# Fetching the rows of eleven steps one by one on SP in a graph network kernel

## The chip, the core and the metric

The kernel runs on one core of a Trainium2 chip. A core has five engines that work side by side, each with its own queue of instructions: TensorE (PE, whose weight loads the profile lists apart as PEld), VectorE (DVE), ScalarE (ACT), GpSimd (POOL) and SyncE (SP). [...] DMAs are issued from these queues too: here SP and ACT issue plain transfers, and POOL issues indirect ones, in which a list of row numbers says where each of 128 rows comes from. The metric is the device time of one execution in microseconds.

## What is computed

There are 6250 nodes with 256 features and 100,000 edges, sorted by their target `dst`; an edge has 64 features. Two layers follow each other, each added to its input and normalised:

```python
e   = relu((x[dst] - x[src]) @ theta_w.T + theta_b + x[src] @ phi_w.T + phi_b)
out = segment_max(e, dst)                  # first layer, 0 where a node has no edge
x   = layernorm(x + out)
...
hv = x @ W_in + b_in                       # second layer, two rounds with own weights W, b
for W, b in ((W_u0, b_u0), (W_u1, b_u1)):
    m   = relu(concat(hv[src], edge_attr) @ W + b)
    msg = segment_max(m, dst)
    hv  = hv + where(has_in, msg, 0)
out = layernorm(x + relu(hv @ W_ro + b_ro))
```

In all three aggregations a node takes the maximum over its incoming edges of a row that depends on the source node alone, plus (in the two rounds) a product of the edge's own features. The part that depends on the source can therefore be computed once for each node and written to a table in DRAM; what remains for each edge is to fetch a row of 1 KB from that table and take part in a running maximum.

## The kernel before

`sweep(r)` makes one of three passes, r = 0 for the first layer and 1 and 2 for the two rounds. The edges are laid out as 128 lanes of 782 steps, so that a step is 128 edges, one on each partition. Steps are gathered in groups of eight (K = 8), and a group has one tile `run` of 128 x 8 x 256 floats, 1 MB, out of a ring of nine such buffers. The steps also form 14 blocks (thirteen of 56 steps, one of 54), within which the running maximum goes on from step to step.

A step goes through these stations:

- **POOL** fetches the 128 source rows from `table[r]` with one indirect DMA into the step's slot of `run` (`sources`, L798). The function `gathered` says how far these gathers run ahead: about 41 steps, five groups. In pass 0, 40 steps take another way and have no gather in this place.
- **PE** computes, in passes 1 and 2, the products of the edge features for two steps at a time (`pair`, L833) from a tile `hT`, which ACT loads for a whole group, three groups ahead (`features`, L822).
- **DVE** adds those products to the fetched rows, two steps at a time (L1043), and takes the running maximum in place, one step at a time (L1056).
- **SP** stores the group's tile of running maxima to `S` in DRAM, 1 MB, when its eight steps are done (L1064).

At a block's end `over_lanes` carries maxima across lanes: PE transposes, ACT copies (`lim2`, L846), DVE scans, and ACT puts the result into `cs` (L865).

The 49 node tiles of a pass are placed between the steps by a plan worked out when the program is built. For each, POOL fetches the rows of `S` at which the tile's nodes end (`rows`, L878), and this gather waits for all S stores issued up to then. Then DVE and PE add what came in from other lanes (`picks`, L890, and `carried`, L897), DVE takes the maximum (L944), ACT the relu (L945), and products with the next weights follow (transposes L768, the copy `aT` on ACT L770, the product L776, `new` L956). ACT then stores the new rows into the next pass's table. SP loads `x` and `xT` for these tasks (L902, L906).

The plan fixes each engine's order. SP's queue thus holds an S store for each group and few things besides, POOL's holds the gathers, and ACT's holds the hT loads, the stores to the tables and to the output, and the small operations of node tiles and blocks.

The buffers of `run` are handed out by the pool in the order in which the tiles are asked for: the ninth request after a tile gets its buffer, and what writes there first waits until the store of the old content is done. Before the change a tile is asked for when the first gather of its group is issued (in `sources`).

Of the kernel before, what the change touches and what calls it, by code (L numbers as in the profile page):

```python
# [8 lines left out]
F32 = mybir.dt.float32  # L9
BF16 = mybir.dt.bfloat16  # L10
I32 = mybir.dt.int32
AF = mybir.ActivationFunctionType
OP = mybir.AluOpType
# [4 lines left out]
P = 128  # L18
N = 6250
D = 256  # L20
# [3 lines left out]
K = 8  # L24
# [19 lines left out]
TROWS = ROWS + 1  # L44
# [3 lines left out]
FIRM = K  # L48
AHEAD = 5 * K
RING = 9  # L50
KEPT = 7
SLACK = 600

# [15 lines left out]
def raw(s):  # L69

    i = s // K * 2 + s % K
    return i if s % K < 2 and i < RAW else None
# [13 lines left out]
def place(t):  # L86

    return P * (t - 1) if t else SPARE + 1
# [376 lines left out]
@with_exitstack  # L465
def gnn_kernel(
    ctx: ExitStack, tc: tile.TileContext, x, xT, src, dst, he, th_wT, th_b, ph_wT, ph_b,
    w_in, b_in, w_u0, b_u0, w_u1, b_u1, w_ro, b_ro, pos, heT, xTn, xn, w_inT, head, near, out,
):
    nc = tc.nc  # L470
    const = ctx.enter_context(tc.tile_pool(name="const", bufs=1))
    dram = ctx.enter_context(tc.tile_pool(name="dram", bufs=1, space=DRAM))
    table = [dram.tile([TROWS, D], F32, name=f"table{r}") for r in range(3)]
# [19 lines left out]
    part = const.tile([P, 1], F32)  # L493
# [18 lines left out]
    wt = const.tile([P, 2, D], F32)  # L512
    s_s = const.tile([P, FS], I32)
    s_r = const.tile([P, RAW], I32)
    s_e = const.tile([P, EARLY], I32)
    whole = const.tile([P, NB], F32)
    lim = const.tile([P, FS], F32)
# [3 lines left out]
    with tc.manual_schedule(), tc.tile_pool(name="pro", bufs=2) as pro, \  # L521
            tc.tile_pool(name="pro_ps", bufs=4, space=PSUM) as pps:
        nc.sync.dma_start(wd, ph_wT.rearrange("(k p) f -> p k f", p=P))
        nc.scalar.dma_start(wt, th_wT.rearrange("(k p) f -> p k f", p=P))
        dp = pro.tile([P, 2 * FS], I32, name="dp", bufs=1)
        d_s, p_s = dp[:, :FS], dp[:, FS:]
        nc.scalar.dma_start(s_r, near)
        for i in range(SOON):
            gather_raw(nc, x, h_sb, s_r, i)
        zero = pro.tile([1, D], F32, name="zero", bufs=1)  # L530
        nc.vector.memset(zero, 0.0)
        for r in range(3):
            nc.scalar.dma_start(table[r][SPARE:SPARE + 1, :], zero)
        parts = []
        for g in range(NT // PART):
            xg = pro.tile([P, 2, PART * P], F32, name="xg", bufs=NT // PART)
            nc.sync.dma_start(xg, xTn[:, :, g * PART * P:(g + 1) * PART * P])
            parts.append(xg)
            if g == 0:
                nc.sync.dma_start(dp, pos[:, 4 * NB:4 * NB + 2 * FS])  # L540
                nc.sync.dma_start(ends_sb.rearrange("p a b -> p (a b)"), pos[:, :4 * NB])
                nc.sync.dma_start(s_s, pos[:, 4 * NB + 2 * FS:])
        nc.vector.tensor_sub(wd, wd, wt)

        def check():
            down = pro.tile([P, FS], F32, name="down", bufs=1)
            nc.vector.tensor_tensor(down, p_s, d_s, OP.is_lt)
            downs = pro.tile([P, 1], F32, name="downs", bufs=1)
            nc.vector.tensor_reduce(downs, down, AX.X, OP.max)
            out_of = pro.tile([1, 2, NB], F32, name="out_of", bufs=1)  # L550
            nc.vector.tensor_tensor(out_of[:, 0, :], fd[0:1, :], floor, OP.is_lt)
            nc.vector.tensor_tensor(out_of[:, 1, :], fd[0:1, :], ceil, OP.is_gt)
            bad = pro.tile([1, 1], F32, name="bad", bufs=1)
            nc.vector.tensor_reduce(bad, out_of.rearrange("p a b -> p (a b)"), AX.X, OP.max)
            nc.vector.tensor_max(downs[0:1, :], downs[0:1, :], bad)
            breaks_p = pps.tile([P, 512], F32, name="breaks_p", bufs=1)
            nc.tensor.matmul(breaks_p[:, :1], every, downs, start=True, stop=True)
            nc.vector.tensor_copy(breaks, breaks_p[:, :1])
            keep = pro.tile([P, FS], F32, name="down", bufs=1)
            nc.vector.tensor_tensor(keep, p_s, d_s, OP.is_equal)  # L560
            alike = BLOCKS.count(BLOCKS[0])
            nc.vector.tensor_reduce(whole[:, :alike], keep[:, :alike * BLOCKS[0]].rearrange(
                "p (b s) -> p b s", s=BLOCKS[0]), AX.X, OP.min)
            for b in range(alike, NB):
                nc.vector.tensor_reduce(whole[:, b:b + 1], keep[:, FIRST[b]:FIRST[b] + BLOCKS[b]], AX.X, OP.min)
            nc.vector.tensor_scalar(lim, keep, 2.0 * BIG, -BIG, OP.mult, OP.add)
            bits = pro.tile([P, FS], I32, name="bits", bufs=1)
            nc.vector.tensor_scalar(bits, s_s, float(P), float(TROWS), OP.is_lt, OP.mult)
            nc.vector.scalar_tensor_tensor(s_s, s_s, float(-P), bits, OP.add, OP.add)
            nc.vector.tensor_scalar(s_e, s_s[:, :EARLY], float(SPARE), None, OP.min)  # L570
            nc.vector.tensor_scalar(bits, d_s, P - 1, None, OP.bitwise_and)
            nc.vector.tensor_copy(lo, bits)
            nc.vector.tensor_scalar(bits, d_s, 7, None, OP.arith_shift_right)
            nc.vector.tensor_copy(hi, bits)

        for g, xg in enumerate(parts):
            g0 = pro.tile([P, PART, D], F32, name="g0", bufs=3)
            for i in range(0, PART, 2):
                w = min(2, PART - i)
                ps = pps.tile([P, 512], F32, name="ps0")  # L580
                for q in range(w):
                    for k in range(2):
                        nc.tensor.matmul(ps[:, q * D:(q + 1) * D], xg[:, k, (i + q) * P:(i + q + 1) * P], wd[:, k, :],
                                         start=(k == 0), stop=(k == 1))
                put = g0[:, i:i + w, :].rearrange("p a f -> p (a f)")
                nc.scalar.copy(put, ps[:, :w * D])
            i = 1 if g == 0 else 0
            if i:
                nc.sync.dma_start(table[0][place(0):place(0) + P, :], g0[:, 0, :])
            at = place(g * PART + i)  # L590
            nc.sync.dma_start(table[0][at:at + (PART - i) * P, :].rearrange("(a p) f -> p a f", p=P), g0[:, i:, :])
            if g == 0:
                check()
# [10 lines left out]
def in_order(ctx: ExitStack, tc: tile.TileContext, g):  # L604
# [8 lines left out]
    nc = tc.nc  # L613
    table, ident, above, every, col, col_f = (g[n] for n in ("table", "ident", "above", "every", "col", "col_f"))
    whole, lim, lo, hi, s_s, fd, pd, ld, nd = (g[n] for n in ("whole", "lim", "lo", "hi", "s_s", "fd", "pd", "ld", "nd"))
    heT, xTn, xn, out = (g[n] for n in ("heT", "xTn", "xn", "out"))
    s_e, head, x, h_sb, wd, s_r, x1 = (g[n] for n in ("s_e", "head", "x", "h_sb", "wd", "s_r", "x1"))
    part = g["part"]
    ctx.enter_context(tc.manual_schedule())
    one = ctx.enter_context(tc.tile_pool(name="one", bufs=1))  # L620
    work = ctx.enter_context(tc.tile_pool(name="work", bufs=2))
# [11 lines left out]

    first = work.tile([P, 4, 2, D], F32, tag="run", name="first", bufs=RING)

# [35 lines left out]
    nc.vector.tensor_scalar(link, whole, 2.0 * BIG, -BIG, OP.mult, OP.add)  # L671
    cs = one.tile([P, KEPT, D + 2], F32, name="cs")
    nc.vector.memset(cs[:, :, D:], 1.0)
# [36 lines left out]
    for i in range(2):  # L710
        low.append(psum.tile([P, 512], F32, tag="he", name="low", bufs=5))
        n = min(half * K, FS - i * half * K)
# [66 lines left out]
    def sweep(r):  # L779
# [9 lines left out]

        runs = ahead.pop(r, {})  # L790

        def sources(s, r=r, runs=runs):
            if s % K == 0:
                runs[s // K] = work.tile([P, K, D], F32, tag="run", name="run", bufs=RING)
            if r == 0 and raw(s) is not None:
                return
            early = r > 0 and s < EARLY
            nc.gpsimd.indirect_dma_start(  # L798
                out=runs[s // K][:, s % K, :], out_offset=None, in_=table[r][:SPARE + 1, :] if early else table[r],
                in_offset=bass.IndirectOffsetOnAxis(ap=(s_e if early else s_s)[:, s:s + 1], axis=0))  # L800

        def raw_turn(i):

# [37 lines left out]
        def over_lanes(b, last):  # L841
# [18 lines left out]
            def back():  # L860
# [3 lines left out]
                carried_in.append(b)  # L864
                nc.scalar.copy(cs[:, b % KEPT, :D], cp[:, :D])  # L865

# [3 lines left out]
        def node(t, g, b):  # L870
# [22 lines left out]
            def carried():  # L893
                assert max(carried_in) - SPAN[t][0] < KEPT
                o["v"] = psum.tile([P, 512], F32, tag="v", name="v", bufs=1)
# [110 lines left out]
        for t in reversed(range(NT)):  # L1006
            e = max(FIRST[SPAN[t][1]] + BLOCKS[SPAN[t][1]], begin)
            b = max(b + (gap if b < FS else 3), e + 4, gathered(e) + 4)
            g = e
# [13 lines left out]
        for s in range(FS):  # L1023
# [4 lines left out]
            c, j = divmod(s, K)  # L1028
# [8 lines left out]
            if s % 2 == 0:  # L1037
# [6 lines left out]
                elif raw(s) is not None:  # L1044
                    sums = hp.pop(s // 2)
                    i = raw(s) // 2
# [7 lines left out]
            row = sums[:, s % 2 * D:(s % 2 + 1) * D]  # L1054
# [10 lines left out]
            if s == FIRST[blk] + BLOCKS[blk] - 1:  # L1065
                over_lanes(blk, prev)
                blk += 1
            for f, a in tasks.pop(s, ()):
                f(*a)
        for f, a in tasks.pop(FS):  # L1070
# [9 lines left out]
    for r in range(3):  # L1080
        sweep(r)
# [50 lines left out]
```

## Time and profile before

| | |
|---|---|
| median of three timed runs | 4156.62 us |
| lowest and highest of them | 4119.23 and 4168.13 us |
| the profiled execution itself | 4196.96 us |
| its span on the core | 4195.2 us |
| mean granted TensorE clock in it | 0.666 |
| busy: POOL, DVE, PE, ACT | 57%, 50%, 46%, 6% |
| S stores of a group (1 MB each) | 291 of 297 |
| data moved | 752.27 MB, 179 GB/s on average |

A row for a group of instructions gives source line, engine, operation, the tiles written and read, the shape, and the count; after the bar come the summed busy time in us and the mean of one in ns; after the second bar the time for which the engine had stood idle just before them, and what ended most of that time ("issue" where nothing in the profile shows a reason, "remote" where it was a semaphore that can't be put down to one instruction). SPq, ACTq and POOLq stand for the queues, in which loads of registers and issues of DMAs are listed. Source lines are those of the kernel before.

The 1.8 us between the span and the profiled time lie around the program. The profiled execution took 1% longer than the median of the timed ones, so sums made from its rows are made against 4196.96 us.

### The profile page before, as it was taken

How to read it: one execution, taken by the hardware profiler on the slowest of the kernel's cores; microseconds unless marked ns; L12 is line 12 of the kernel's file. 1: busy time of each engine (PE TensorE's matmuls, PEld its weight loads, DVE VectorE, ACT ScalarE, POOL GpSimd, SP SyncE). 2: the span in 40 equal slices, each digit the busy share in tenths (PEclk: the TensorE clock that was granted, in tenths of full speed). 3: DMA queues.
4: the chain of work that ended last, by engine and by line, in shares of the span. 5: the costliest groups of instructions: out<-in, count | busy, mean ns of one | idle time of the engine just before them, and what ended most of it. 6: DMA issues, size and time to landing. Idle time of an engine off the chain costs nothing. (4 is left out here: it accounts for less than half of the span.)

```text
span 4195.2 us, 21994 instructions
## 1 busy us (share of the span) xinstructions
PE 1921.7 (46%) x4631; PEld 844.2 (20%) x4631; DVE 2117.7 (50%) x4750; ACT 234.5 (6%) x618; POOL 2382.1 (57%) x2500
## 2 busy tenths in 40 slices
PE   5353223445442244454455455454444555555555
PEld 4232112111110111222211111121122222211111
DVE  1265556444444345455555544454455656555556
ACT  1000000111110000000000000000000000000000
POOL 5554555665556655566565555555555655555553
PEclk8665555655655566777776766677677777666667
DMA  6454546555555555555565555555555655555554
GB/s 232 134 179 145 169 141 211 167 186 182 185 176 205 177 161 181 175 187 188 170 202 172 186 183 172 169 192 176 174 182 180 194 189 194 177 181 178 185 182 154
DMA packets 261984, 752.27 MB, mean 179 GB/s; under 512 B 54725, under 2 KB 116914, under 8 KB 224594
## 3 DMA queue, kind: packets, MB, share of 16 engines
q0 software_dynamic: 119664, 326.92, 26.1%
q1 hardware_dynamic: 82672, 344.28, 22.3%
q10 hardware_dynamic: 59506, 79.59, 5.9%
q8 instruction: 39, 0.64, 0.1%
q14 instruction: 103, 0.84, 0.1%
HBM read 410.98 MB, written 339.59 MB: 179 GB/s over the span
## 5 line engine op out<-in xcount | busy, mean ns | idle before, releaser
L798 POOL DMA_INDIRECT run<-table,s_s x2258 | 2156.2, 955 | 903.4 <-issue 664.4
L833 PE MATMUL hp<-whe,hT 128*128 128x512 f32 x1564 | 1066.4, 775 | 669.2 <-DVE run L1056 244.4
L1056 DVE SCALAR_TENSOR_TENSOR run<-run,lim,hp 128x256 f32<-128x256 f32 x1573 | 754.8, 480 | 309.3 <-remote 128.1
L878 POOL DMA_INDIRECT m<-S,end_i x147 | 140.6, 957 | 833.8 <-DMA S<-run 368.7
L1043 DVE TENSOR_TENSOR hp<-hp,run 128x512 f32<-128x512 f32 x782 | 541.3, 692 | 140.9 <-remote 51.4
L833 PEld LDWEIGHTS hp<-whe,hT 128*128 128x128 f32 x1564 | 303.7, 231 | 1200.2 <-DVE run L1056 495.8
L1056 DVE SCALAR_TENSOR_TENSOR run<-run,lim 128x256 f32<-128x256 f32 x731 | 351.9, 481 | 125.2 <-remote 42.1
L897 PE MATMUL v<-cs,pick 128*128 128x256 f32 (+1 forms) x438 | 184.4, 540 | 258.3 <-issue 92.9
L768 PE MATMUL tp<-ident,h_sb 128*128 128x128 f32 x196 | 52.4, 360 | 416.9 <-DVE h_sb L948 219.9
L776 PE MATMUL prod<-wcat,aT 128*128 128x512 f32 x196 | 178.3, 1064 | 61.2 <-issue 44.0
L944 DVE TENSOR_TENSOR m<-m,v 128x256 f32<-128x256 f32 x98 | 40.6, 414 | 308.6 <-remote 248.0
L718 DVE TENSOR_TENSOR ol<-col,low 128x1024 bf16<-128x1024 bf16 x98 | 118.9, 1213 | 123.5 <-remote 110.3
L897 PEld LDWEIGHTS v<-cs,pick 128*128 128x128 f32 x438 | 105.0, 265 | 370.5 <-issue 260.0
L729 PE MATMUL hist<-oh,ol 128*128 128x8 bf16 (+7 forms) x782 | 34.7, 167 | 314.4 <-DVE oh L724 244.0
L945 ACT ACTIVATE m<-m,has 128x256 f32<-128x256 f32 x98 | 49.8, 508 | 1622.7 <-DVE m L944 1023.2
L768 PEld LDWEIGHTS tp<-ident,h_sb 128*128 128x128 f32 x196 | 24.0, 172 | 516.7 <-issue 471.4
L939 DVE TENSOR_TENSOR new<-prod,b 128x256 f32<-128x256 f32 x49 | 20.8, 424 | 167.8 <-PE prod L776 69.5
L729 PEld LDWEIGHTS <-ol 128*128 128x128 bf16 x782 | 36.0, 103 | 339.8 <-DVE ol L718 246.2
L956 DVE TENSOR_TENSOR new<-prod,bu 128x256 f32<-128x256 f32 x49 | 20.6, 421 | 163.3 <-remote 106.5
L776 PE MATMUL prod<-wu,aT 128*128 128x256 f32 x196 | 72.7, 509 | 60.7 <-ACT aT L770 31.7
L960 DVE TENSOR_TENSOR m<-prod,bro 128x256 f32<-128x256 f32 x49 | 20.7, 422 | 151.5 <-remote 99.2
L768 PE MATMUL tp<-ident,x 128*128 128x128 f32 x98 | 31.6, 424 | 142.7 <-DVE no L916 39.9
(133 smaller groups left out, 1486.0 us busy)
## 6 DMA issues: line engine op xcount, KB each, us to landing
S<-run SPq DMA_DIRECT2D x291, 1024.0 KB
hT<-in_heT ACTq DMA_DIRECT2D x196, 256.0 KB
run<-table,s_s POOLq DMA_INDIRECT x2258
table<-new ACTq DMA_DIRECT2D x98, 128.0 KB
xg<-in_xTn SPq DMA_DIRECT2D x7, 896.0 KB
xT<-in_xTn SPq DMA_DIRECT2D x49, 128.0 KB
x<-in_xn SPq DMA_DIRECT2D x49, 128.0 KB
x<-x ACTq DMA_DIRECT2D x49, 128.0 KB
```

The costliest lines, as they stand in the source:

```text
L718: nc.vector.tensor_tensor(ol[:, :k, :], col.unsqueeze(1).to_broadcast([P, k, P]), low[c // half][:, c % half * K:c % half * K + k].unsquee ...
L729: nc.tensor.matmul(hist[:, t0:t0 + w], ol[:, j, :], oh[:, j, :w], start=False, stop=(c == NG - 1 and j == k - 1))
L768: nc.tensor.transpose(tp[:, k * P:(k + 1) * P], a[:, k * P:(k + 1) * P], ident)
L776: nc.tensor.matmul(ps[:, :n], aT[:, k, :], w[:, k, :], start=(k == 0), stop=(k == 1))
L798: nc.gpsimd.indirect_dma_start(out=runs[s // K][:, s % K, :], out_offset=None, in_=table[r][:SPARE + 1, :] if early else table[r], in_offs ...
L833: nc.tensor.matmul(hp[i], hT[c][:, q, :], whe[r - 1].rearrange("p s f -> p (s f)"), start=True, stop=not early)
L878: i = nc.gpsimd.indirect_dma_start(out=o["m"], out_offset=None, in_=S_r[:P * (FIRST[SPAN[t][1]] + BLOCKS[SPAN[t][1]]), :], in_offset=bass. ...
L897: nc.tensor.matmul(o["v"][:, :N1], p, cs[:, blk % KEPT, :N1], start=(blk == SPAN[t][0]), stop=(blk == SPAN[t][1]))
L944: nc.vector.tensor_max(o["m"], o["m"], o["v"][:, :D])
L945: nc.scalar.activation(o["m"], o["m"], AF.Relu, scale=has[:, t:t + 1])
L1043: nc.vector.tensor_add(sums, sums, two)
L1056: nc.vector.scalar_tensor_tensor(cur, prev, lim[:, s:s + 1], row, OP.min, OP.max)
```

## The change

Eleven steps of each pass, named in `SIDE`, are the last steps of groups 10, 18, 26 and so on up to 90. POOL no longer gathers these: 33 gathers of the three passes are gone. Their 128 rows are fetched by SP in eight parts of sixteen. At the first step of every group from 2 to 89, behind the S store of the group before, SP loads sixteen row numbers from a small tile `side_sb` into registers, and then issues sixteen DMAs, each of which copies one row of 1 KB from the table to its partition of the step's slot. The eight parts of a step are thus spread over the eight groups ahead of its own. The tiles of these groups are asked for at the first part (`place_for`), because the slot must exist by then; before, a tile was asked for about five groups ahead.

The row numbers are prepared in the prologue, in the same way as those of the gathers: one more load by SP, and two small DVE operations. In this text `FusedRegOps` or FUSED_REGOPS is the instruction by which SP works out a DMA's address from the register.

```diff
+SIDE = [(8 * i + 10) * K + K - 1 for i in range(11)]
...
+    side_sb = const.tile([len(SIDE), P], I32)
...
+                nc.sync.dma_start(side_sb, side)
...
+            nc.vector.tensor_scalar(bits_b, side_sb, float(P), float(TROWS), OP.is_lt, OP.mult)
+            nc.vector.scalar_tensor_tensor(side_sb, side_sb, float(-P), bits_b, OP.add, OP.add)
...
+        def place_for(c, runs=runs):
+            if c not in runs:
+                runs[c] = work.tile([P, K, D], F32, tag="run", name="run", bufs=RING)
+
         def sources(s, r=r, runs=runs):
             if s % K == 0:
-                runs[s // K] = work.tile([P, K, D], F32, tag="run", name="run", bufs=RING)
-            if r == 0 and raw(s) is not None:
+                place_for(s // K, runs)
+            if r == 0 and raw(s) is not None or s in SIDE:
                 return
...
+        def rows_one_by_one(i, part_of):
+
+            s, n = SIDE[i], P // K
+            regs = [nc.sync.alloc_register(name=f"row{r}_{i}_{part_of}_{q}") for q in range(n)]
+            nc.sync.load(regs, side_sb[i:i + 1, part_of * n:(part_of + 1) * n])
+            for q, reg in enumerate(regs):
+                number = nc.sync.snap(reg, donate=True, min_val=0, max_val=TROWS - 1)
+                p = part_of * n + q
+                nc.sync.dma_start(runs[s // K][p:p + 1, s % K, :], table[r][bass.ds(number, 1), :])
...
+            if j == 0:
+                for i, to_come in enumerate(SIDE):
+                    if 0 < to_come // K - c <= K:
+                        for ahead_c in range(c + 1, to_come // K + 1):
+                            place_for(ahead_c)
+                        rows_one_by_one(i, K - (to_come // K - c))
             for f, a in tasks.pop(s, ()):
                 f(*a)
```

In program order the batch of a group thus stands on SP behind the store of the group before, and ahead of the loads of `x` and `xT` that belong to the same step. The orders of PE, ACT and DVE are otherwise the same, and POOL's differs by the missing gathers.

## The prediction

> **What bounds the kernel now.** I read the page first: the engines' busy rows, then the costliest groups, then the waits, then stretches of a pass. In the groups the last pair of columns is busy time with the mean of one, and idle time ahead with what ended most of it.
>
> ```profile
> PE 1921.7 (46%) x4631; PEld 844.2 (20%) x4631; DVE 2117.7 (50%) x4750; ACT 234.5 (6%) x618; POOL 2382.1 (57%) x2500
> ...
> L798 POOL DMA_INDIRECT run<-table,s_s x2258 | 2156.2, 955 | 903.4 <-issue 664.4
> L878 POOL DMA_INDIRECT m<-S,end_i x147 | 140.6, 957 | 833.8 <-DMA S<-run 368.7
> L1056 DVE SCALAR_TENSOR_TENSOR run<-run,lim,hp 128x256 f32<-128x256 f32 x1573 | 754.8, 480 | 309.3 <-remote 128.1
> L1043 DVE TENSOR_TENSOR hp<-hp,run 128x512 f32<-128x512 f32 x782 | 541.3, 692 | 140.9 <-remote 51.4
> ```
>
> No engine is full. POOL comes nearest: a gather is 0.955 us busy, and in the timeline the next starts 1.25 us after it (0.30 us "issue" between). All 2493 gathers make 3116 us of a span of 4195.2; most of POOL's other time is the 834 us ahead of the m gathers. There it waits for S stores:
>
> ```profile
> POOL m L878 <- DMA S<-run: 368.7, 29, 28.3
> ```
>
> So POOL has run ahead and waits for what DVE has just computed: it is not the last one. The gathers do run far ahead of DVE: `gathered` allows about 41 steps.
>
> What paces DVE shows in the windows (columns: PE, PEld, DVE, ACT, POOL busy, then granted clock, DMA share, GB/s):
>
> ```profile
> 2089.00:2123.00 34.00, 23.35 (x54) 8.14 (x52) 30.41 (x63) 1.76 (x4) 22.05 (x24) 1.00 0.84 290
> 2123.00:2198.00 75.00, 35.81 (x77) 15.96 (x77) 33.83 (x72) 4.14 (x11) 40.78 (x44) 0.68 0.48 156
> ```
>
> A pass alternates. In fast stretches DVE is 89% busy (30.41 of 34.00) at full clock, and a group of 8 steps takes 4 x (0.69 + 2 x 0.48) = 6.6 us. In slow ones the granted clock falls (0.68 here, 0.50 in the 58 us after), DVE is 45% busy and waits at node ends for PE, up to 24 us at a time ahead of L944. Through both, SP mostly waits for DVE. The next lines are SP's largest wait, from the waits of its own queue, and ten S stores of a fast stretch, from its timeline (start, length, count):
>
> ```profile
> SPq L1064 <- DVE run L1056: 1746.1, 132, 60.9
> ```
> ```profile
> 1538.74 60.77 SPq L1064 DMA_DIRECT2D S<-run  x10
> ```
>
> Nine intervals in 60.45 us are 6.7 us each. Over the 267 groups in which the change adds work (2 to 90 of each pass), the start times of L1064 give intervals of 3604 us in sum, 13.5 us on average; 143 of them are under 11 us. SP has little to do, but the change gives it a batch per group.
>
> **Removed.** 33 gathers on POOL (11 steps x 3 passes): 33 x 1.25 = 41 us of POOL's time. As POOL waits for DVE's stores, I take 0 on the path; bounds 0 and -41. The bytes stay: the same rows move.
>
> **Added on SP.** Behind each of 88 stores a pass: one load of 16 registers, 16 address computations, 16 DMAs of one row (1 KB). In all 264 loads, 4224 computations, 4224 DMAs, against some 500 DMAs on SP now. Nearest rows, from the views of two source lines (min/median/max ns):
>
> ```profile
> L595 SPq TENSOR_LOAD <-breaks x1: 510/510/510, 48.0 to 48.0; - x1
> L595 SPq FUSED_REGOPS  x1: 191/191/191, 48.6 to 48.6; - x1
> ```
> ```profile
> L533 ACTq DMA_DIRECT2D table<-zero x3: 233/313/592, 1.8 to 2.7; - x3
> ```
>
> The last is a DMA of one row too, and its issue costs what that of a 1 MB S store costs (0.320 us). Gaps between SP's instructions are about 0.06 us. A row is 0.191 + 0.313 + 0.06 = 0.56 us, 16 rows 9.0 us; with the store (0.32 us) and the load (0.51 us) a batch is B = 9.9 us.
>
> [...] The trace has loads of one register only[...]. By the row the sum below is about +110 us[...]. I take 0.6 us more than the row[...]: B = 10.5 us.
>
> The ring adds a wait: tiles for eight groups ahead are taken at once, so the first batch of every eight writes into the buffer whose S store was just issued, and SP stands until that has landed. In the trace's DMA records stores land 4.1 us after issue (mean; 3.4 to 5.3), so 33 batches take some 3.8 us more, 0.5 us on the average of all: B = 11. Lowest: if address and issue overlap, a row is 0.35 us; row eight of a batch waits for the store's landing anyway (below), so 4.1 + 9 x 0.35 = 7.3 us.
>
> **Who waits for SP.** The plain DMAs of SP and ACT share eight completion semaphores, taken in program order, and each waits until the one eight before it has landed. In the program after the change row 8 of a batch waits for the store, rows 9 to 16 for rows 1 to 8, and ACT's next transfer (the hT load of group c+3 at the start of group c) for the rows of the batch before. Behind that load in ACT's queue stand relu (L945), the aT copy (L770), lim2 (L846), cs (L865). So SP's lateness reaches PE through hT, and DVE through the last rows of the SIDE step. The hT load for c+3 waits for about the tenth row of batch c-1, which begins with group c-1; PE needs it when DVE begins group c+2, three groups or 19.8 us later. Ten rows of sixteen take 7 us and the landing 2 to 3 us, as the trace's small loads do, so SP may be late by about 10 us before DVE slows; 6 us if the last rows and landings take longer.
>
> **The sum.** I replay the 267 intervals: each store begins when DVE is ready or B after the one before, whichever is later, and what its lateness exceeds the tolerated lag by is added to DVE's delay. In lockstep (no lag) B = 9, 10, 11, 13 adds 201, 313, 446, 756 us; with 6 us of lag 68, 145, 241, 495; with 10 us 43, 79, 153, 378. For B = 11 I take the middle of 241 and 153: +197 us. The slow stretches hide the rest; were their cover gone, the lockstep figure would hold.
>
> ACT's 196 stores of table, x1 and out are also held inside a batch: at most 8 rows x 0.56 = 4.5 us, half on average, in 11 of 13.5 us: 196 x 2.25 x 0.8 = 353 us as upper bound, 0 as lower. Node tasks stand 6 steps apart and mostly absorb it: a tenth, +35 us. The prologue's one load and two small DVE operations on 11x128 cost under 1 us of DVE beside PE's start: 0 to +2, taken as 0. PE's instructions stay.
>
> Sum: 4197 (profiled run, 4195.2 span and 1.8 around it) + 197 + 35 = 4429 us. The median of the timed runs is 4156.62, 0.990 of the profiled run: 4429 x 0.990 = 4385 us.
>
> **Rivals.**
> A. Absorbed (the other side: not slower). Slow stretches come with a low granted clock after PE-heavy bursts. If that limits PE's average work, a burst slowed by SP is paid back by a shorter slow stretch. For: clock 1.00 in bursts, 0.5 to 0.68 between, on a total of PE work that doesn't change. Against: in the slow stretches node chains wait on each other, not on matmul throughput alone. It also decides where B is near 7.3 us: the replay gives under +75. Time 4157 to 4230, say 4180.
> B. Faster. Smoothed bursts let the clock stay high, and POOL's 41 us come off the path where it catches up. 4157 - 41 = 4116 from POOL alone; over 2% needs another 42 us of the clock. Against: DVE doesn't wait for gathers in the trace.
> C. Lockstep with costly loads. B = 13 and no tolerance gives +756, with 6 us of lag +495. For: ACT and SP are coupled in every group. 4157 + 0.99 x 495 = 4647, up to 4905; say 4700.
>
> **How the numbers follow.** The main case has 0.43 (4250 to 4500: with B from 10 to 12 at 10 and 6 us of lag +79 to +357, the ACT term 0 to 100); A 0.30, of which 0.04 above 4240; B 0.09; C 0.18. Two per cent (83 us) is about what a measurement of this kernel tells from no change, its runs spread by 1.2%. Faster by over 2% (under 4073): 0.08, from B. Within 2%: 0.27, from A and the rest of B. Slower: 0.65. The range leaves out most of B below 4105 and the upper part of C above 4800.
>
> **What would show it.** SP's rows: 4224 row DMAs of about 0.31 us and computations of 0.19; the 16-register load at 0.5 to 1.1 us (main)[...]. Store starts in fast stretches 10 to 12 us apart instead of 6.7; SP's wait for DVE falls far below 1746 us; PE's wait for hT and ACT's for DMAs appear; POOL's 2225 run gathers stay at 0.955 us and wait longer. The granted clock tells A: if it rises in the slow stretches and these shorten, the bursts were paid back. I am wrong if a row costs 0.35 us or less, if PE is truly limited on average, or if ACT's held stores reach the node chains in full.

## The result, and the profile after

The kernel after the change takes 5202.43 us (5200.02 to 5214.46), the kernel before beside it 4141.57 us: 1.256 times as long, with a 95% interval of 1.248 to 1.265. The direction was forecast and the size was not: 1061 us were lost where some 230 were expected, outside the range.

One thing has to be said ahead of all numbers. The experiments ran on several chips, and these are of two kinds: on some the kernel before takes 4141 to 4181 us, as in the runs above, on others 3179 us. Each experiment is therefore compared with the kernel before on its own chip. In the following the two kinds are called the slower and the quicker chips. Each chip of the experiments ran one batch of them and none came back, so whether the chip itself makes the difference, or something that held during its batch, the runs don't show.

The first rows are from the page of the kernel after: busy time by engine, then two groups with busy time, mean ns of one, and the idle time ahead with its main releaser. Line numbers are those of the kernel after: L808 are the gathers, L1063 the add, L1076 the running maximum, L1084 the S store, L816 the load of the sixteen row numbers, L820 the row DMAs.

```profile
PE 1871.7 (36%) x4631; PEld 850.9 (16%) x4631; DVE 2112.4 (41%) x4752; ACT 234.6 (5%) x618; POOL 2355.8 (45%) x2467
...
L808 POOL DMA_INDIRECT run<-table,s_s x2225 | 2128.8, 957 | 1253.1 <-issue 656.8
...
L1063 DVE TENSOR_TENSOR hp<-hp,run 128x512 f32<-128x512 f32 x782 | 541.0, 692 | 943.2 <-DMA run<-table 667.5
```

The engines are busy for about as long as before and wait longer. DVE's add now waits 667.5 us for rows of `run`. The waits of SP's own queue show who is late now:

```profile
SPq L1084 <- DVE run L1076: 217.8, 39, 54.0
SPq L820 <- DMA hT<-in_heT: 83.2, 45, 5.7
```

SP waited 1746 us for DVE before; of that 218 us are left. SP has become the engine on which the others wait. Its trace keeps one order throughout: in all 264 batches the store comes first, then the load, then the sixteen rows, and none of its 13,880 instructions starts before the one ahead has ended. Its instructions are listed by the views of two lines (min/median/max ns):

```profile
L816 SPq TENSOR_LOAD <-side_sb x264: 354/2747/3864, 158.3 to 5117.7; - x132
```
```profile
L820 SPq FUSED_REGOPS  x4224: 1/37/1397, 160.6 to 5130.6; - x192
L820 SPq MOVE run<-table x4224: 1/29/1403, 161.9 to 5130.7; - x192
L820 SPq DMA_DIRECT2D run<-table x4224: 1/228/1408, 161.9 to 5130.8; - x192
```

By the medians a row is 0.41 us with the gaps between instructions, and a whole undisturbed batch 9.8 to 10.4 us (store 0.36, load 2.75, sixteen rows 6.6), a little less than forecast. But the columns of extremes reach 1.4 us, even for a MOVE; 404 of the 4224 MOVEs last between 0.6 and 0.8 us. The timeline of SP shows both cases (start, length, count):

```profile
4283.22 41.36 SPq L820 DMA_DIRECT2D run<-table  x16
4324.68 0.35 SPq L1084 DMA_DIRECT2D S<-run  x1
4328.04 6.43 SPq L820 DMA_DIRECT2D run<-table  x16
```

The same sixteen rows took 41.36 us in one batch and 6.43 us in the next. Two stretches of the same time show what differed (PE, PEld, DVE, ACT, POOL busy and counts, clock, DMA share, GB/s):

```profile
4281.00:4318.00 37.00, 0.54 (x2) 0.00 (x0) 0.00 (x0) 0.00 (x0) 28.12 (x30) 0.57 0.42 131
4318.00:4329.00 11.00, 0.00 (x0) 0.00 (x0) 0.00 (x0) 0.00 (x0) 0.00 (x0) 0.50 0.28 108
```

In the slow batch POOL issued gather after gather. Its last gather ended at 4318; the slow batch went on to 4324.6, and the next one ran at full speed. Over all 267 groups with a batch or its neighbour, the starts of the stores lie 4665 us apart in sum (17.5 us each), where it was 3604 us before (13.5 us each): the whole loss is there. The sixteen rows of all 264 batches, from the start of the first to the end of the last, take 3553 us in sum, where 264 undisturbed ones of 6.4 us would take 1690.

### The profile page after: what moved, and what is told of

Its sections match the earlier page's. It is cut to its first block, busy times and chain, and to the rows that moved or that the text cites. A ratio compares the mean times of both kernels' runs of the same rounds, so it can differ in the third digit from the quotient of the medians.

```text
span 5212.7 us, 34850 instructions
## 1 busy us (share of the span) xinstructions
PE 1871.7 (36%) x4631; PEld 850.9 (16%) x4631; DVE 2112.4 (41%) x4752; ACT 234.6 (5%) x618; POOL 2355.8 (45%) x2467
## 5 line engine op out<-in xcount | busy, mean ns | idle before, releaser
L808 POOL DMA_INDIRECT run<-table,s_s x2225 | 2128.8, 957 | 1253.1 <-issue 656.8
L853 PE MATMUL hp<-whe,hT 128*128 128x512 f32 x1564 | 1008.7, 740 | 1359.5 <-DVE run L1076 1231.8
L1063 DVE TENSOR_TENSOR hp<-hp,run 128x512 f32<-128x512 f32 x782 | 541.0, 692 | 943.2 <-DMA run<-table 667.5
L1076 DVE SCALAR_TENSOR_TENSOR run<-run,lim,hp 128x256 f32<-128x256 f32 x1573 | 754.7, 480 | 88.9 <-issue 19.9
L1076 DVE SCALAR_TENSOR_TENSOR run<-run,lim 128x256 f32<-128x256 f32 x731 | 351.5, 481 | 97.1 <-DMA run<-table 60.4
L917 PE MATMUL v<-cs,pick 128*128 128x256 f32 (+1 forms) x438 | 173.4, 516 | 336.7 <-DVE pick L910 227.4
L981 DVE SCALAR_TENSOR_TENSOR m<-m,x 128x256 f32<-128x256 f32 x49 | 20.8, 425 | 425.3 <-DMA x<-x 398.5
L782 PE MATMUL prod<-wt,xT 128*128 128x256 f32 x196 | 98.3, 655 | 257.7 <-DMA xT<-in_xTn 248.5
L932 DVE TENSOR_TENSOR h_sb<-prod,tb 128x256 f32<-128x256 f32 x49 | 20.7, 423 | 272.7 <-PE prod L782 238.1
L944 DVE TENSOR_TENSOR m<-m,x 128x256 f32<-128x256 f32 x49 | 20.7, 422 | 268.1 <-DMA x<-in_xn 267.1
L868 PE MATMUL lp<-ident,run 128*128 128x128 f32 x84 | 24.2, 383 | 214.8 <-DVE run L1076 180.1
L782 PEld LDWEIGHTS prod<-wt,xT 128*128 128x128 f32 x196 | 56.0, 315 | 277.4 <-DMA xT<-in_xTn 259.2
L873 DVE TENSOR_TENSOR_SCAN cT<-lim,cT,lp 128x128 f32<-128x128 f32 x78 | 33.2, 468 | 157.0 <-PE lp L868 109.5
```

Of the source, the lines that this page charges most:

```text
L782: nc.tensor.matmul(ps[:, :n], aT[:, k, :], w[:, k, :], start=(k == 0), stop=(k == 1))
L808: nc.gpsimd.indirect_dma_start(out=runs[s // K][:, s % K, :], out_offset=None, in_=table[r][:SPARE + 1, :] if early else table[r], in_offs ...
L853: nc.tensor.matmul(hp[i], hT[c][:, q, :], whe[r - 1].rearrange("p s f -> p (s f)"), start=True, stop=not early)
L873: nc.vector.tensor_tensor_scan(to[:, k, 1:], lim2, lp[:, k * P:(k + 1) * P], of[:, k, P:] if b else 0.0, OP.min, OP.max)
L917: nc.tensor.matmul(o["v"][:, :N1], p, cs[:, blk % KEPT, :N1], start=(blk == SPAN[t][0]), stop=(blk == SPAN[t][1]))
L1063: nc.vector.tensor_add(sums, sums, two)
```

## Experiments

Four theories were set against each other as the runs went on. I: SP gets through its instructions more slowly while POOL gathers without a pause. T: each row DMA itself is held for some 4 us. B: the undisturbed length of SP's batch is enough to explain the loss. S: that length together with SP's waits for ACT's transfers is enough. Kernels with fixed or neighbouring rows put rows into the steps that are not theirs; they serve for their times alone.

**First four, on a quicker chip (before: 3179 us).** Fixed row addresses:

```diff
-            regs = ...; nc.sync.load(regs, side_sb[i:i + 1, part_of * n:(part_of + 1) * n])
-                nc.sync.dma_start(runs[s // K][p:p + 1, s % K, :], table[r][bass.ds(number, 1), :])
+                nc.sync.dma_start(runs[s // K][p:p + 1, s % K, :], table[r][p:p + 1, :])
```

> Sixteen row DMAs a batch stay, but with fixed addresses: no load of registers, no address computation, so a row is one instruction of SP instead of three (the SIDE steps get rows that are not theirs). In the trace after the change a row takes 0.41 us when POOL pauses and up to 4.2 us late in an unbroken run of POOL's gathers. Theory I (instructions: during such runs SP gets only an instruction per 0.7 to 1.4 us): rows of 0.3 us in pauses, about 1.3 us in runs, batches of 5 to 21 us, time 4150 to 4350 us. Theory T (each row DMA itself is held for about 4 us): rows still near 4 us in runs, time 4700 to 5000 us. Theory B (only the length of an undisturbed batch counts): batches of 5 us, below nearly all store intervals, time 4130 to 4170 us.

Measured: 3144 us, ratio 0.989 (0.988 to 0.991). 4224 row DMAs cost nothing here, so T falls on this chip.

One DMA for a SIDE step:

```diff
+            if part_of == 0:
+                nc.sync.dma_start(runs[s // K][:, s % K, :], table[r][:P, :])
```

> The 33 gathers are gone as in the change and the tiles are taken early as in the change, but each SIDE step is filled by a single DMA of 128 neighbouring rows (rows that are not its own): SP gets 33 DMAs in place of 4224. All theories of SP's batches: 4100 to 4142 us, the gain being at most the 41 us of POOL's time. If taking eight tiles early is what costs (the ring), it is well above 4142.

Measured: 3138 us, 0.987 (0.986 to 0.989), a gain of 41 us, as much as 33 gathers of 1.25 us. On this chip POOL is the bound, which its row of busy tenths shows (0.955 of every 1.25 us is a busy share of 7 tenths):

```profile
POOL 6777777777777777777777777777777777777775
```

Rows into a tile that nobody reads:

```diff
-            if r == 0 and raw(s) is not None or s in SIDE:
+            if r == 0 and raw(s) is not None:
...
-                nc.sync.dma_start(runs[s // K][p:p + 1, s % K, :], table[r][bass.ds(number, 1), :])
+                nc.sync.dma_start(aside[0][p:p + 1, :], table[r][bass.ds(number, 1), :])
```

> POOL keeps all its gathers as before; SP does the loads, address computations and row DMAs of the change, but into a tile that nobody reads, and the ring's tiles are taken as before. Theories I and T (SP itself is too slow, and S stores and the shared completion semaphores carry it on): 5000 to 5250 us, as with the change. If it is the SIDE step's wait for its own rows that costs (667 us of DVE's wait ahead of the add): 4400 to 4550 us.

Measured: 3972 us, 1.249 (1.247 to 1.251). Nobody waits for these rows, and the loss is there: here it is SP's queue, not the SIDE step's data. But SP's instructions are even, in gathers and out of them, which speaks against I on this chip:

```profile
L823 SPq MOVE aside<-table x4224: 29/29/42, 91.7 to 3909.0; - x192
```

Over a third of the gathers replaced by plain DMAs from ACT's queue, with the change in place:

```diff
+            if s % 2 and s % K < K - 1 and s >= EARLY:
+                nc.scalar.dma_start(runs[s // K][:, s % K, :], table[r][P:2 * P, :])
+                return
```

> The change, and in addition the gathers of the odd steps from 24 on, other than the last of a group, are replaced by one plain DMA each of 128 neighbouring rows, issued by ACT (those steps get rows that are not theirs): POOL has some 1100 gathers fewer, and its unbroken runs are shorter. Theories I and T (POOL's runs starve SP): rows of over 1 us become rare, a batch takes 10 to 12 us on average instead of 17.7, time 4300 to 4500 us. Theory B (length of the batch alone): the batches were no longer than 10.3 us anyway and the time stays near 5200 us. ACT's 1100 DMAs of about 0.35 us each are a new load (390 us of ACT's queue, which is mostly idle); they share completion semaphores with SP's rows and may add to the time.

Measured: 3900 us, 1.227 (1.223 to 1.231). Against I again on this kind of chip, as there was nothing to relieve: no MOVE of SP took over 42 ns here either. It is even slower than the change alone (1.192, k2 below); SP waited 411 us for ACT's usual transfers and 303 us for transfers into `run`, to which ACT's row DMAs now belong.

**The parts of the change, on a slower chip (before: 4175 us).** The change once more:

> The kernel after the change, once more, beside its parts. With the rows into a tile that nobody reads the ratio was 1.249 on a chip where the kernel before took 3179 us; there an undisturbed batch was 9.8 us (store 0.36, load 2.76, sixteen rows of 0.41), and SP's rows waited 3.1 us more on average for transfers that ACT had issued. Theory S (SP's own time plus these waits, 13 to 14 us a group, against some 10.5 us that POOL needs for one): ratio 1.22 to 1.27. If the SIDE steps' wait for their own rows adds to it: above 1.30.

Measured: 5240 us, 1.257 (1.251 to 1.263), as at first.

The load without the computations, and the computations without the loads:

```diff
+                if q == n - 1:          # as with the change
...
+                else:
+                    nc.sync.dma_start(runs[s // K][p:p + 1, s % K, :], table[r][p:p + 1, :])
```

> The load of sixteen registers stays in every batch, but only the last row of a batch takes its address from one; the other fifteen have fixed addresses (rows that are not theirs). A batch is 0.36 + 2.76 + 15 x 0.29 + 0.41 = 7.9 us of SP, some 11 with lane waits as they were. Theory S: ratio 0.99 to 1.06. If the load itself is the cost, through the time that SP stands still in it: 1.10 to 1.20. Theory I (number of SP's instructions): 17 fewer of three parts, ratio 0.99.

```diff
+            if not once:
+                nc.sync.load(regs, ...)
+                once.extend(nc.sync.snap(reg, min_val=0, max_val=TROWS - 1) for reg in regs)
+            for q, number in enumerate(once):
```

> The registers are loaded once in a pass and used by every batch (rows that are not theirs): 261 of 264 loads are gone, the 4224 address computations and row DMAs with register addresses stay. A batch is 0.36 + 16 x 0.41 = 6.9 us of SP, about 10 with lane waits. Theory S: ratio 0.98 to 1.03. Theory I (the number of SP's instructions, 48 a batch as with the change): 1.15 to 1.25. If the load is the cost: 0.99.

Measured: 4833 us, 1.159 (1.153 to 1.165), and 4919 us, 1.179 (1.173 to 1.185). Theory S gave at most 1.06 and 1.03 and falls on this kind of chip: batches of 7.9 and 6.9 us of SP's own time should have fitted. The first ratio lies where it was expected if the load is the cost (1.10 to 1.20), and far from the 0.99 that theory I gave by the number of instructions alone; the second lies in the range of I (1.15 to 1.25), where the load as the cost would have given 0.99. So neither the load nor the number of instructions explains both. The timeline of the first, g2, has the pattern again: fifteen rows of one instruction each in 13.11 us, while a run of gathers ends, and in 4.45 us a moment later.

```profile
2004.04 13.11 SPq L823 DMA_DIRECT2D run<-table  x15
...
2021.15 4.45 SPq L823 DMA_DIRECT2D run<-table  x15
```

Half of each batch on ACT:

```diff
+            for e, (eng, name) in enumerate(((nc.sync, "sp"), (nc.scalar, "act"))):
+                p0 = part_of * n + e * n // 2
+                eng.load(regs, side_sb[i:i + 1, p0:p0 + n // 2])
```

> The change with half of every batch on ACT's queue: SP and ACT each load eight registers and issue eight rows (the right ones). SP's batch is 0.36 + 1.5 + 8 x 0.41 = 5.1 us, about 8 with lane waits, below POOL's 10.5. Theory S: SP is no longer the last, ratio 0.98 to 1.05. If waits between ACT's and SP's transfers are what costs, rather than SP's own time, they get worse, since ACT's rows stand behind its relu and copies, which wait for DVE and PE up to 90 us: ratio 1.15 to 1.40.

Measured: 4644 us, 1.113 (1.107 to 1.118). This is better than the change, above what S allows (1.05), just below what was expected if the waits between ACT's and SP's transfers are the cost (1.15), and still a loss.

From these traces it can be worked out what a row takes by how long POOL's gathers have run unbroken when it is issued (time from one row DMA's start to the next, median in us; a run is broken where over 0.6 us lie between two gathers):

| kernel, chip | instructions per row | 0 to 5 us | 20 to 30 us | 40 to 60 us |
|---|---|---|---|---|
| after, slower | 3 | 0.41 | 3.50 | 4.20 |
| load, fixed rows (g2), slower | 1 | 0.30 | 1.40 | 1.40 |
| fixed rows (h1, below), slower | 1 | 0.30 | 1.40 | 1.40 |
| after (k2, below), quicker | 3 | 0.41 | 0.41 | 0.41 |

Late in a run SP gets through one instruction per 1.4 us, be it a DMA, a MOVE or an address computation: three of them make 4.2 us. With half of the rows on ACT (g5) a row late in a run takes 4.20 us on SP and 4.20 us on ACT: each of the two queues is held to this pace by itself. The slowing starts earlier than the table's columns say: in the kernel after, the median row of a batch takes 1.05 us at 5 to 10 us of a run and 2.12 us at 15 to 20. This is theory I, now as a pace and not as a count of instructions, and it holds on the slower chips alone.

**Tests of that cause, on a slower chip (before: 4144 us).** Fixed rows as in the first experiment:

> Sixteen rows of fixed addresses per batch again (not the SIDE steps' own), since the chip decides so much: where the kernel before took 3179 us the ratio was 0.989. Theory I, as it now stands: on chips where the kernel before takes some 4170 us, an engine gets only one instruction per 1.4 us once POOL's gathers have run unbroken for some 20 us; a batch of 17 instructions, 5 us long undisturbed, takes some 24 us there. Against 34 instructions with a load in the batch (ratio 1.159) and 50 (1.257) that gives 1.04 to 1.12 on such a chip, and 0.99 again on the other kind. If only the length of undisturbed batches counts: 0.99 on both.

Measured: 4507 us, 1.088 (1.084 to 1.092). The same kernel gained 1% on a quicker chip. Both are as theory I had it (1.04 to 1.12 here, 0.99 there). The issue itself has the same median in both traces, 0.25 us; what differs is the time from one row's start to the next late in a run, 1.40 us here (table) and 0.30 us there.

The kernel before with fewer gathers (the edit of the fourth experiment):

> The kernel before, with the gathers of the odd steps from 24 on, other than the last of a group, replaced by one plain DMA of 128 neighbouring rows each, issued by ACT (rows that are not theirs): POOL has some 870 gathers fewer. Theory I (POOL's unbroken runs starve the other engines of instructions): on a chip of the 4170 us kind 3000 to 3600 us, DVE and PE keeping their pace; on the 3179 us kind, where POOL itself sets the pace, 2500 to 3000. If the slow stretches come from PE's limited clock: on the 4170 us kind no gain beyond 3%, 4050 to 4250.

Measured: 3161 us, 0.763 (0.761 to 0.765) and within the forecast of theory I (3000 to 3600 us). POOL had 838 gathers fewer. PE had the same instructions and 1778 us of busy time (1922 before); the thousand microseconds were not PE's limit. The edit does two things at once, though: it breaks up POOL's runs, and it takes 838 x 1.25 = 1048 us of work off POOL.

```profile
PE 1778.3 (56%) x4631; PEld 802.7 (25%) x4631; DVE 2104.4 (67%) x4750; ACT 234.1 (7%) x618; POOL 1589.3 (50%) x1662
```

The same with the change:

> The change together with those fewer gathers (SIDE steps as in the change; odd steps get rows that are not theirs). On the 3179 us kind of chip this took 3900 us, 1.227 times the kernel before. Theory I: on the 4170 us kind SP's batches come near their undisturbed 10.3 us plus lane waits, 12 to 14 us instead of 17.7, and the time near that of the other kind, 3800 to 4200 us. If the starvation comes from SP's own stream and not from POOL: 5000 to 5200 us.

Measured: 4492 us, 1.084 (1.081 to 1.087), where the change alone has 1.257, which speaks for I, but 300 us above what was expected. The slowing became less and did not go: few rows are now issued over 20 us into a run, but at 5 to 10 us the median row takes 1.18 us, and the rows of all batches still take 2935 us in sum, against 1690 undisturbed and 2449 for the same kernel on the quicker chip.

A smaller ring, nothing else:

```diff
-RING = 9
+RING = 6
```

> The kernel before with a ring of six tiles in place of nine, nothing else: a gather may write a tile only when the store of the one six groups earlier has landed, so POOL pauses more often and its unbroken runs get shorter, without any gather being taken away. Theory I: on the 4170 us kind faster, 3700 to 4100 us; on the 3179 us kind, where POOL has no time to pause, 3180 to 3300 us. If POOL's runs are not the cause: 4170 us or slower, as a wait is added and nothing removed.

Measured: 3985 us, 0.959 (0.953 to 0.966). A wait was added (POOL stands idle 1398 us in all ahead of its run gathers, 903 before), no gather taken away, and the kernel got faster, within the 3700 to 4100 us of theory I. This separates what the fewer gathers mixed. Added up over POOL's runs, the time beyond the first 20 us of each is 1578 us in the kernel before, 1383 with the ring of six and 593 with fewer gathers: 195 and 985 us less, while the time fell by 159 and 984 us. That the second pair agrees so closely is partly chance, as the slowing starts before 20 us and is not total.

**The second term, on a quicker chip (before: 3179 us).** The hT loads from SP instead of ACT:

```diff
-            nc.scalar.dma_start(hT[c].rearrange("p q e -> p (q e)"), heT[c])
+            nc.sync.dma_start(hT[c].rearrange("p q e -> p (q e)"), heT[c])
```

> The change with the 196 hT loads issued by SP, between the store and the batch, instead of by ACT. If SP's waits for ACT's transfers are a term of their own: SP's rows no longer wait for hT (392 of 811 us of such waits on the 3179 us kind of chip), and in spite of 0.35 us more of SP per group the time falls below that of the change, by 100 to 250 us. If SP's own instructions are all that counts: the time rises by 0 to 70 us (196 x 0.35).

> The kernel after the change, as the reference of this chip: ratio 1.25 to 1.26 on the 4170 us kind; on the 3179 us kind near 1.25, as with the rows into a tile of their own, if the SIDE step's wait for its own rows costs nothing more; above 1.30 if it does.

> The load of sixteen registers and fifteen fixed rows a batch, as before (rows not the SIDE steps' own): 1.16 again on the 4170 us kind. On the 3179 us kind, where SP's instructions aren't slowed, 7.9 us a batch plus waits stays within POOL's 10.5 us: 0.99 to 1.04.

Measured: 3705 us, 1.165 (1.163 to 1.167), for hT on SP; 3790 us, 1.192 (1.190 to 1.195), for the change itself, less than either of its forecasts; 3565 us, 1.121 (1.119 to 1.124), for the load with fixed rows. SP's waits with the change, then with hT on SP:

```profile
SPq L820 <- DMA hT<-in_heT: 261.5, 124, 6.4
...
SPq L820 <- DMA table<-new: 145.4, 60, 5.7
SPq L820 <- DMA x<-x: 97.1, 43, 6.2
SPq L820 <- DMA out<-new: 88.5, 38, 5.5
```
```profile
SPq L820 <- DMA table<-new: 175.8, 70, 5.8
...
SPq L820 <- DMA x<-x: 96.1, 43, 6.2
SPq L820 <- DMA out<-new: 58.5, 32, 4.5
```

The waits fell from 592 to 330 us; the 196 issues cost SP 69 us, and the 264 loads took 3.32 instead of 2.94 us on average, 99 us more. That leaves 94 us, and the time fell by 85, just short of the 100 expected. So the waits for ACT's transfers are a real but smaller term. On the quicker chip SP's batch of some 10 us and 2.2 us of such waits (592 us over 264 batches) come near the 12.9 us that a group takes there, against some 10.5 us that POOL needs for one. The load with fixed rows was forecast at up to 1.04, and missed: SP waited 790 us for ACT's transfers, 3.0 us a batch, which with 7.9 us is 10.9, above POOL's pace. Why the rows into an unread tile cost more (1.249) than the change (1.192) is not settled; SP's waits for ACT's transfers were 811 us there, and POOL kept its 33 gathers.

A ring of five with gathers 32 steps ahead, here and on a slower chip (before: 4181 us), where the single DMA was repeated too:

```diff
-AHEAD = 5 * K
-RING = 9
+AHEAD = 4 * K
+RING = 5
```

> The kernel before with a ring of five tiles and gathers 32 steps ahead in place of nine and 40, nothing else. If short runs of gathers are what speeds up the 4170 us kind: at or below the 0.959 of the ring of six, 0.88 to 0.96. If the later gathers make DVE wait instead: 0.97 to 1.05. On the 3179 us kind, where POOL never pauses, 1.00 to 1.08.

> The kernel before with a ring of five tiles and gathers 32 steps ahead once more. On the 3179 us kind 1.00 again. On the 4170 us kind: 0.88 to 0.96 if shorter runs of gathers are what counts, at or below the ring of six (0.959); 0.97 to 1.05 if the later gathers make DVE wait.

> The 33 gathers removed and each SIDE step filled by one DMA of 128 neighbouring rows (rows that are not its own), as once before. On the 3179 us kind of chip 0.987 again, 41 us, POOL being the last there. On the 4170 us kind, where POOL pauses for 1080 us in all, the prediction's reading (POOL waits for DVE's stores) gives 1.000; if shorter runs of gathers also mean less slowing of the other engines, 0.98 to 0.99.

Measured: the ring of five 3187 us, 1.003 (1.002 to 1.003), on the quicker chip and 4053 us, 0.971 (0.967 to 0.976), on the slower one; the single DMA 4168 us, 0.998 (0.996 to 1.000), on the slower one. The ring of five was to be at or below 0.959 if short runs are what counts, and was not: its 0.971 lies at the edge of the other forecast (0.97 to 1.05), in which DVE waits for the later gathers. Its runs were no shorter than with the ring of six, 1393 us beyond the first 20 us, so it doesn't test shorter ones. Of the kernels that fetch the right rows, the ring of six is the fastest seen on a slower chip; on a quicker one it was not run.

## Why the prediction was wrong

**The step that failed** is "The slow stretches hide the rest". The replay let SP need the same B = 11 us everywhere, so that its lateness from fast stretches would be worked off in slow ones. In truth the slow stretches are where POOL gathers without a pause, and there SP itself slows, to 1.4 us per instruction late in a run. The sixteen rows of a batch take 6.4 us undisturbed; their median is 11.0, and in a tenth of the batches they take 25 to 42 us. In sum they take 3553 us instead of 1690, of which SP's waits for ACT's transfers (below) make 224. On the quicker chip, where no MOVE of SP took over 42 ns, the same sum is 2308 us, and SP's waits there (592) are nearly all of its excess. So SP lost time exactly where it was to catch up. The prediction's own figure for the cover gone, 446 us in lockstep at B = 11, falls short for the same reason: B was not 11 there. Rival C came nearest in time (4700, up to 4905) for another reason: its 13 us a batch were the author's assumption, with no load of more than one register in the trace to show them, and an undisturbed batch takes 9.8 to 10.4.

**Behind it stands a wrong reading of the kernel before.** The fast and slow stretches were put down to PE and its granted clock. Here are three stretches of its trace once more, cut along POOL's gathers: a pause of POOL, the first 20 us of a run, and the rest of that run.

```profile
2152.00:2172.00 20.00, 13.17 (x35) 7.27 (x35) 13.01 (x31) 2.36 (x7) 0.00 (x0) 0.70 0.40 143
2172.00:2192.00 20.00, 14.76 (x34) 6.59 (x32) 16.46 (x35) 1.78 (x5) 14.88 (x16) 0.83 0.69 232
2192.00:2247.00 55.00, 19.30 (x22) 4.61 (x20) 16.90 (x32) 0.00 (x0) 41.60 (x45) 0.56 0.56 181
```

DVE issues 31 and 35 instructions in the first two stretches of 20 us, and 32 in the 55 us after them: one per 1.7 us. PE goes from 35 matmuls in 20 us to 22 in 55. Two other runs of POOL in this trace are like it (41 instructions of DVE in 20 us, then 32 in 54; 41 in 20, then 41 in 52). The timeline late in the run shows who waits for whom:

```profile
2205.81 0.70 DVE L1043 TENSOR_TENSOR hp<-hp,run 128x512 f32<-128x512 f32 x1 [3.21 <-PE hp L833]
2206.55 1.00 DVE L1056 SCALAR_TENSOR_TENSOR run<-run,lim,hp 128x256 f32<-128x256 f32 x2
2207.60 2.08 PE L833 MATMUL hp<-whe,hT 128*128 128x512 f32 x2 [2.86 <-issue]
2211.40 0.70 DVE L1043 TENSOR_TENSOR hp<-hp,run 128x512 f32<-128x512 f32 x1 [3.86 <-issue]
```

DVE does its add and two maxima at their usual lengths and then stands until PE's next products are there: in this stretch the trace holds PE's signal for four of the adds, and each starts 0.02 to 0.03 us after it. The adds come every 4.9 to 6.3 us, 5.6 on average; at 2186 to 2191 us they still came every 1.64 us. So the prediction was right that DVE waits for PE, and wrong on why PE is slow: at the low clock the two matmuls of a pair take 2.08 us, far less than 5.6. Two weight loads and two matmuls in 5.6 us are again one instruction per 1.4 us, as on SP. Breaking up the runs alone (ring of six, 0.959) brought part of the pace back. Cutting the trace where PE was slow hid this, and cutting it where POOL starts and stops would have shown it before any change was made. Rivals A and B both built on the clock and fall with it; the mean clock of the kernel after is 0.644, not higher than the 0.666 before.

**The batch.** Its length of 11 us was right by two errors that cancel. A row of three instructions takes 0.41 us undisturbed, not 0.56: the address computation is 0.037 us (the single instance in the trace before had 0.191), the MOVE 0.029, the DMA 0.228 (0.313) and each of the three gaps some 0.04 (0.06). The load of sixteen registers takes 2.75 us at the median, not the 1.1 us taken: (2.75 - 0.51) / 15 = 0.15 us for each further register, where the 0.6 us added to the row of a single register, an estimate, left 0.04. The extra wait for the S store at the first batch of eight, 3.8 us, does not appear: the list of SP's waits in the kernel after has none for an S store. POOL's run gathers are the ones that wait for stores, 180.1 us in 17 waits.

**ACT's stores.** They were to be held by SP's rows, for 35 us. The wait that SP's list shows runs the other way: SP's rows wait for ACT's transfers, 224 us on the slower chip (hT 83.2, out 58.0, table 52.7, x 29.8) and 592 us on the quicker. The tolerated lag of 6 to 10 us left this out, since it had SP only as the one who makes others wait. How much ACT lost to SP's rows was not worked out.

**What held.** Removing 33 gathers is worth nothing on a slower chip (0.998), as POOL pauses there anyway (1067 us in all in the kernel before, counting pauses of over 0.6 us); on a quicker one it is worth the full 41 us. That SP would turn from the one who waits into the one waited for, that the stores in fast stretches would come 10 to 12 us apart (10.4 and 11.5 from 2408.56 us on), and that the shared semaphores would tie ACT and SP together, all show in the trace. The 4712 plain DMAs of SP and the 412 of ACT signal the same eight semaphores there, 640 or 641 times each, and 4208 of the 4224 row DMAs wait on the one that they then signal. The row that shares the store's is the eighth in 128 of the 264 batches and the fifth to seventh in 133. Of the two ways by which SP's lateness was to reach the others, only one shows much: DVE waits for the rows of the SIDE steps (667.5 us), while PE's waits for hT are 28.0 us in all, 17.6 before.

**How the loss splits** on slower chips, by ratios: 4224 row DMAs with fixed addresses 1.088; with the loads 1.159; with the address computations 1.179; with both 1.257. The three parts nearly add up: 8.8 + 7.1 + 9.1 = 25.0 against 25.7 per cent (8.8 for the row DMAs, 7.1 more with the loads, 9.1 more with the computations instead). On quicker chips the row DMAs cost nothing, the loads bring it to 1.121 and the computations to 1.192.

## What to carry to other kernels

An idle queue is not free capacity (here 12,936 instructions on a queue that had waited 1746 us for DVE cost 1061 us): count the instructions, address arithmetic and register loads included, that a change puts on it per period, and find out how fast that queue runs in the very stretches that are meant to hide it. Where a kernel alternates between fast and slow stretches, cut its trace along the activity of each engine in turn, not only of the one that looks slow. And before a long run of gathers on POOL is taken for harmless work in the background, try how the kernel fares when it is broken up (0.959 here, with the ring of six).

## What the runs showed of the hardware

On the slower chips, while POOL's indirect DMAs run without a pause, other engines slow down: SP's median row of three instructions goes from 0.41 us to 1.05 at 5 to 10 us of a run, and to 4.20 at 40 to 60, one instruction per 1.4 us. SP shows this in all of these traces, ACT's queue where it issues rows too (g5), and PE by its pace in the trace of the kernel before (two weight loads and two matmuls in 5.6 us); DVE there waits for PE and runs at its usual speed in between (0.70 us an add and 1.00 for two maxima in the lines shown, against means of 0.69 and 0.48 each). The slowing ends within some us of POOL's pause: in the batch shown about 6 us after the last gather, and of the rows issued 3 to 6 us after one, 6% take over 1 us. On the quicker chips SP's rows took 0.30 us deep inside a run of gathers of 2219 us (fixed rows, e1), and in the traces with register addresses no MOVE took over 42 ns. The amount of data alone does not account for it: where plain DMAs fetched as many bytes in place of 838 of the gathers (neighbouring rows, though, not scattered ones; 752.25 MB in h2, 752.27 before), the slowing became less (h3: the rows of all batches take 2935 us in sum, 3553 after the change alone).

What is shared between POOL's gathers and the other engines' instructions, and why chips differ, these runs don't show. That instructions come late to the engines would be a guess, and the trace of the kernel after doesn't support it. Its slow MOVEs last 0.70 us themselves, with about as long (0.69 us) between them and their neighbours. The queue that its page lists as `instruction` (q14) had 100 packets more (203 against 103) for some 12,900 more instructions, one packet for about 130; more than 10 us into POOL's runs these packets took a median of 0.32 us, in its pauses 0.38. Nor do the runs show whether an execution without the profiler is slowed in the same way: each execution of the experiments on record has a span and a granted clock.
